# A list scheduler's durations refitted, TensorE's changes of tile shape counted, and strips of two key blocks joined in layers 2 and 3

## The chip, the cores and the metric

The kernel runs on one core of a Trainium2 chip. The metric is the device time of one launch in microseconds, the median of several runs. Everything is computed in float32.

## The reference

A batch of 32 samples x of 512 nodes by 256 features passes through four graph-attention layers. All samples share one 512 x 512 adjacency matrix. Each layer takes h = relu(layernorm(x)) and adds its result to x.

- Layer 0: multi-head attention, 4 heads of 64. Scores q k / 8, masked by the adjacency, softmax, times v, an output projection.
- Layer 1: a linear layer to 512 with relu, a graph attention without mask over 512 features, a linear layer back to 256 with relu, a second graph attention with the mask, elu and relu.
- Layer 2: graph attention with 4 heads of 64. The score of nodes i, j is leaky_relu(s_i + d_j), masked, softmax over j, times the projected features; then elu.
- Layer 3: the same with 8 heads of 32 and a prior beta * log(adj + eps) added to the score, then an output projection.

## The kernel before, in words

**Tiles.** A sample is worked in blocks of 128 partitions x 512 columns of float32. There are 61 such SBUF buffers (`BLOCKS`), 8 PSUM banks, 4 buffers for x, and some small ones. NT = 4 is the number of 128-node blocks, KD = 2 and KH = 4 the numbers of 128-feature blocks of 256 and 512.

**The shapes on TensorE.** Most matmuls use the whole 128 x 128 array, with 512 or 256 to 272 columns streamed. Some use a part of it, several side by side:

- `sc` in layer 0 (scores of two heads): 64 rows each, two side by side, in one unit of two matmuls.
- `av` in layers 0 and 2 (weighted sum of v): 64 output columns each, two side by side.
- `av` in layer 3, `sm` (sums of the softmax's denominators) in layers 0, 2 and 3, and `f1p` in layer 1: 32 output columns each, four side by side.

**Layers 2 and 3** (`separable`): the softmax's numerator of head h, key block j is max(R, e) * mask, one scalar_tensor_tensor on VectorE (512 columns) into a block `p3`; R is the row of the other node's score, broadcast to all partitions by a DMA out of a DRAM tile `rd`, which a DMA before it filled from `rT`. For a group of four heads and one key block j, four such products make a strip. Its four `av` and four `sm` matmuls are one unit.

**The order.** Nothing is issued while the layers are written down. `Plan` records each operation of all 32 samples as a `Step`, with its engine, how long it is taken to keep the engine busy and how long until others can use its result (`cost`), and what must come before it. `with q.unit(busy):` joins several matmuls in one step with a duration of its own. `Plan.order` then lists the steps: again and again it takes, over all five engines, the open step that can start first, ties by `due`, the sample's number times `PERIOD` less the length of what still hangs on the step. A step can start when its engine is free (`at`), its inputs are there (`ready`: the producer's end plus `HOP`) and buffers are free (`slots`). At most 4 samples are in work at once (`AHEAD`). `Plan.issue` issues the steps in this order, each on its engine's queue, so every planned instruction has the line L217 in the profile. At run time each engine goes through its queue in order, with semaphores for what it depends on. The planned durations steer only the order.

**The norm** at the head of each layer (`norm_t`): four bn_stats and bn_aggr on VectorE, a small add, `rs` = (var + eps) ** -0.5 as a pow on POOL, four scalings into `h` on VectorE, eight transposes on TensorE into `pt`, two relu copies on ScalarE into `hT`.

Ahead of the planned part some 100 us go to loading weights, testing bounds and making the masks.

Of the kernel before, what the change touches and what calls it, by code (L numbers as in the profile page):

```python
# [14 lines left out]
ALU = mybir.AluOpType  # L15
# [21 lines left out]
SAFE_PRIOR = 20.0  # L37


PERIOD = 90.0  # L40
BLOCKS, KEEP = 61, 12
KEEP_BANKS = 0

# [1 line left out]
class Step:  # L45


    def __init__(self, engine, busy):
        self.engine, self.busy, self.calls = engine, busy, []
        self.touches, self.before, self.after = [], [], []  # L50


class Plan:
# [6 lines left out]


    ENGINES = dict(tensor="PE", vector="DVE", scalar="ACT", gpsimd="POOL", sync="SP")
    HOP, AHEAD = 0.12, 3

    def __init__(self, nc, period):
        self.nc, self.period = nc, period
# [13 lines left out]
        self.samples.append([])  # L80
        self.history = {}

    def unit(self, busy):

        return _Unit(self, busy)

    def add(self, attribute, engine, op, args, kw):
        steps = self.samples[-1]
# [27 lines left out]
    def order(self):  # L116

        owners, left = {}, {}
        for s, steps in enumerate(self.samples):
            for step in steps:  # L120
                step.sample = s
                step.waits = len(step.before)
                step.ready = 0.0
                for name in step.touches:
                    left[name] = left.get(name, 0) + 1
                    owners[name] = s
            for step in reversed(steps):
                step.tail = step.lasts + max((n.tail + self.HOP for n in step.after), default=0.0)
                step.due = s * self.period - step.tail

                if step.engine != "PE" and any(self.tile_tag[name] == "bank" for name in step.touches):
                    step.due -= 1000.0
        free = {tag: [0.0] * bufs for tag, (bufs, _) in self.tags.items()}
        held = {}
        to_come = [{} for _ in self.samples]
        for name, s in owners.items():
            tag = self.tile_tag[name]
            to_come[s][tag] = to_come[s].get(tag, 0) + 1
        live, at = set(), {e: 0.0 for e in self.ENGINES.values()}
        open_ = {e: [] for e in at}  # L140
        for steps in self.samples:
            for step in steps:
                if not step.waits:
                    open_[step.engine].append(step)
        result, count = [], sum(map(len, self.samples))
        oldest = 0

        def slots(step):

            when, taken = 0.0, {}  # L150
            for name in step.touches:
                if name in live:
                    continue
                tag = self.tile_tag[name]
                keep = self.tags[tag][1]
                reserve = 0
                for s in range(oldest, step.sample):
                    if to_come[s].get(tag, 0):
                        reserve += max(0, min(keep, to_come[s][tag] + held.get((s, tag), 0)) - held.get((s, tag), 0))
                n = taken.get(tag, 0)  # L160
                if len(free[tag]) - n <= reserve:
                    return None
                when = max(when, sorted(free[tag])[n])
                taken[tag] = n + 1
            return when

        while len(result) < count:
            best = None
            for engine, waiting in open_.items():
                for step in waiting:  # L170
                    if step.sample > oldest + self.AHEAD:
                        continue
                    start = max(at[engine], step.ready)
                    if best is not None and self.key(start, step) >= best[0]:
                        continue
                    when = slots(step)
                    if when is None:
                        continue
                    start = max(start, when)
                    if best is None or self.key(start, step) < best[0]:  # L180
                        best = self.key(start, step), start, step
            assert best is not None, "the buffers do not suffice"
            _, start, step = best
            step.start = start
            open_[step.engine].remove(step)
            at[step.engine] = start + step.busy
            end = start + step.lasts
            for name in step.touches:
                tag, s = self.tile_tag[name], step.sample
                if name not in live:  # L190
                    live.add(name)
                    free[tag].remove(min(free[tag]))
                    held[s, tag] = held.get((s, tag), 0) + 1
                    to_come[s][tag] -= 1
                left[name] -= 1
                if not left[name]:
                    live.discard(name)
                    held[s, tag] -= 1
                    free[tag].append(end + self.HOP)
            for n in step.after:  # L200
                n.waits -= 1
                n.ready = max(n.ready, start + step.busy if n.engine == step.engine == "PE" else end + self.HOP)
                if not n.waits:
                    open_[n.engine].append(n)
            result.append(step)
            while oldest < len(self.samples) and not any(to_come[oldest].values()) and not any(
                n for (s, _), n in held.items() if s == oldest
            ):
                oldest += 1
        self.makespan = max(at.values())  # L210
        return result
# [15 lines left out]


class _Unit:
    def __init__(self, plan, busy):  # L230
        self.plan, self.busy = plan, busy

    def __enter__(self):
        self.plan.joined = Step("PE", self.busy)

    def __exit__(self, *_):
        self.plan.joined = None
# [14 lines left out]

def cost(engine, op, args, kw, out):

    n = 1
    for _, k in out.ap[1:]:
        n *= k
    if engine == "PE":
        if op == "transpose":
            return 0.11, 0.2  # L260
        return max(0.22, n * 0.00168), 0.2
    if engine == "ACT":
        return 0.08 + 0.00093 * n, 0.09 + (0.19 if "accum_out" in kw else 0.0)
    if engine == "DVE":
        if op == "reciprocal":
            return 0.07 + 0.00625 * n, 0.09
        return 0.066 + 0.00105 * n + (0.06 if op == "scalar_tensor_tensor" and n == N else 0.0), 0.09
    if engine == "POOL":
        return (1.05 if n < 16 else 0.2 + 0.0015 * n), 0.1
    return 0.1, 3.5  # L270


# [1 line left out]
def gnn_stack_kernel(ctx: ExitStack, tc: tile.TileContext, a: dict, out: bass.AP):  # L274
# [218 lines left out]
    def pipelined(stack):  # L493
# [135 lines left out]
        def layer0(xt):  # L629
# [15 lines left out]
            for m in range(KD):  # L645
                av, sm = bank("av"), bank("sm")
                for jj in range(0, NT, 2):
                    p = {}
                    for j in (jj, jj + 1):
                        sc = [bank("sc"), bank("sc")]  # L650
                        with q.unit(0.96):
                            for s, r in enumerate(rows):
                                q.tensor.matmul(sc[s], kT[m][r, col(j)], qT[m][r, :], start=True, stop=True)
                        for s in range(2):
                            p[j, s] = b = block("p0")
                            q.scalar.activation(b, sc[s], AF.Exp)
                            q.vector.tensor_tensor(b, b, mask0T[:, j, :], op=ALU.mult)
                    with q.unit(2.75):
                        for j in (jj, jj + 1):
                            for s, r in enumerate(rows):  # L660
                                q.tensor.matmul(
# [14 lines left out]
        def first_gat(o1):  # L676
# [3 lines left out]

            part, sd = block("part"), small("sd", NT, 2)
            f1p = bank("f1p")
            with q.unit(1.0):
                for k in range(KH):
                    q.tensor.matmul(f1p[k * 32 : k * 32 + 32, :], fr1a[:, k, :], o1[k], start=True, stop=True)
            q.scalar.copy(part, f1p)
# [116 lines left out]
        def separable(xt, w, nh, mask, bars):  # L803
# [23 lines left out]
            for g in range(nh // 4):  # L827
# [2 lines left out]
                    q.sync.dma_start(R[s], rd[4 * g + s : 4 * g + s + 1, :].to_broadcast([P, N]))  # L830
                avs = [bank("av") for _ in range(4 // per)]
                sm = bank("sm")
                for j in range(NT):
                    p = blocks("p3", 4)
                    for s in range(4):
                        h = 4 * g + s
                        q.vector.scalar_tensor_tensor(
                            p[s], R[s], e[:, j, nh + h : nh + h + 1], mask[:, j, :], op0=ALU.max, op1=ALU.mult
                        )
                    st = dict(start=(j == 0), stop=(j == NT - 1))  # L840
                    with q.unit(1.92 if per == 4 else 2.85):
                        for s in range(4):
                            h, r0 = 4 * g + s, s % per * f
                            q.tensor.matmul(avs[s // per][r0 : r0 + f, :], half(v, j)[:, h * f : (h + 1) * f], p[s], **st)
                        for s in range(4):
                            h = 4 * g + s
                            q.tensor.matmul(
                                sm[s * F3 : (s + 1) * F3, :], wj[:, j, h : h + 1].to_broadcast([P, F3]), p[s], **st
                            )
                bars(g, avs, sm)  # L850

# [457 lines left out]
```

## Time and profile before

| | us |
|---|---|
| median of 3 runs | 4729.1 |
| lowest and highest | 4728.43, 4732.22 |
| the profiled execution's own time | 4727.03 |
| its span, first to last instruction | 4725.2 |
| TensorE busy | 4491.1 |
| VectorE busy | 3061.7 |
| ScalarE busy | 1642.7 |
| POOL busy | 611.8 |

The profile is of one execution. PE is TensorE's matmuls, PEld its weight loads, DVE VectorE, ACT ScalarE, POOL GpSimd and SP the queue that issues the DMAs. A row of the groups names the line, the engine, the operation and its tiles as out<-in with the rows*columns of the array, then the number of instructions; after the bar come the busy time and the mean length of one. A float32 matmul shows as two instructions (two passes), a transpose as one. In the waits, "A <- B" says that A's engine stood idle until B was done.

### The profile page before, as it was taken

How to read it: one execution, taken by the hardware profiler on the slowest of the kernel's cores; microseconds unless marked ns; L12 is line 12 of the kernel's file. 1: busy time of each engine (PE TensorE's matmuls, PEld its weight loads, DVE VectorE, ACT ScalarE, POOL GpSimd, SP SyncE). 2: the span in 40 equal slices, each digit the busy share in tenths (PEclk: the TensorE clock that was granted, in tenths of full speed). 3: DMA queues.
4: the chain of work that ended last, by engine and by line, in shares of the span. 5: the costliest groups of instructions: out<-in, count | busy, mean ns of one | idle time of the engine just before them, and what ended most of it. 6: DMA issues, size and time to landing. Idle time of an engine off the chain costs nothing.

```text
span 4725.2 us, 55985 instructions
## 1 busy us (share of the span) xinstructions
PE 4491.1 (95%) x20146; PEld 2069.3 (44%) x20146; DVE 3061.7 (65%) x6772; ACT 1642.7 (35%) x3508; POOL 611.8 (13%) x648
## 2 busy tenths in 40 slices
PE   2999999999999999999999999999999999999986
PEld 1444444444444444444444444444444444444442
DVE  5357676665667665677657776567666675667664
ACT  1343333333333333333333333333333333333321
POOL 1011111011101111111011110111110111101110
PEclk9999999999999999999999999999999999999997
DMA  2001111101111111111111111111011111111111
GB/s 85 10 18 50 34 46 38 43 30 37 38 40 35 44 39 30 46 44 37 35 36 34 44 46 37 33 38 49 28 44 31 41 42 45 29 39 35 42 36 42
DMA packets 168209, 183.04 MB, mean 39 GB/s; under 512 B 64370, under 2 KB 99956, under 8 KB 167924
## 3 DMA queue, kind: packets, MB, share of 16 engines
q1 hardware_dynamic: 161972, 173.10, 12.1%
q10 hardware_dynamic: 5408, 4.20, 0.3%
q8 instruction: 161, 2.64, 0.2%
q0 software_dynamic: 544, 2.10, 0.1%
q14 instruction: 124, 1.02, 0.1%
HBM read 159.92 MB, written 19.40 MB: 38 GB/s over the span
## 4 chain that ended last, share of the span: by engine, by line
PE 82%; DVE 10%; POOL 2%; ACT 2%; DMA 2%; issue 1%; SPq 0%; POOLq 0%; DVEq 0%; ACTq 0%
PE mm L217 34%; PE av L217 26%; PE sm L217 10%; PE pt L217 6%; PE sc L217 4%; DVE stats L217 2%; DVE x L217 2%; POOL rs L217 1%; DVE p L217 1%; DVE h L217 1%; PE f1p L217 1%; POOL p L217 1%; DVE ue L217 1%; DVE yT L217 1%; ACT e L217 1%
## 5 line engine op out<-in xcount | busy, mean ns | idle before, releaser
L217 PE MATMUL av<-p,v 128*128 128x512 f32 (+1 forms) x2048 | 726.2, 603 | 0.1
L217 DVE SCALAR_TENSOR_TENSOR p<-R,e,mask3T 128x512 f32<-128x512 f32 x1024 | 690.8, 748 | 14.3 <-DMA R<-rd 13.9
L217 PE MATMUL av<-p,vs 128*32 128x512 f32 (+1 forms) x3072 | 555.8, 604 | 14.1 <-DVE p L217 13.4
L217 PE MATMUL mm<-W_fc,o 128*128 128x512 f32 x1024 | 484.7, 602 | 0.0
L217 POOL TENSOR_TENSOR rs<-ve,mhalf 128x4 f32<-128x4 f32 x128 | 172.6, 1351 | 2087.1 <-DVE ve L217 1654.7
L217 PE MATMUL sm<-p,w 128*32 128x512 f32 x3072 | 424.8, 597 | 0.0
L217 DVE TENSOR_TENSOR p<-p,mask0T 128x512 f32<-128x512 f32 x512 | 348.1, 717 | 103.6 <-ACT p L217 102.6
L217 DVE SCALAR_TENSOR_TENSOR p<-R,e,mask1T 128x512 f32<-128x512 f32 x512 | 346.6, 748 | 80.1 <-DMA R<-rd 79.8
L217 ACT ACTIVATE p<-sc 128x512 f32<-128x512 f32 x512 | 274.8, 601 | 349.5 <-PE sc L217 348.0
L217 PEld LDWEIGHTS av<-p,v 128*128 128x128 f32 (+1 forms) x2048 | 243.4, 163 | 319.1 <-issue 274.4
L217 PEld LDWEIGHTS av<-p,vs 128*32 128x32 f32 (+1 forms) x3072 | 125.0, 118 | 369.8 <-issue 207.2
L217 POOL TENSOR_SCALAR p<-p,r 128x512 f32<-128x512 f32 x128 | 140.8, 1110 | 1103.2 <-DVE r L217 736.5
L217 PE MATMUL sc<-qT,kT 64*128 64x512 f32 x1024 | 280.9, 634 | 1.1 <-ACT s L217 0.9
L217 PEld LDWEIGHTS mm<-W_fc,o 128*128 128x128 f32 x1024 | 179.9, 190 | 183.1 <-issue 173.6
L217 PE MATMUL mm<-w,hT 128*128 128x272 f32 (+1 forms) x1024 | 255.8, 396 | 2.2 <-ACT hT L217 1.5
L217 DVE TENSOR_SCALAR h<-x,mv,rs 128x256 f32<-128x256 f32 x512 | 215.8, 475 | 62.0 <-POOL rs L217 61.6
L217 PE MATMUL mm<-o,mlp_w 128*128 128x512 f32 x512 | 235.0, 600 | 8.7 <-DVE o L217 8.7
L217 PE MATMUL pt<-ident,h 128*128 128x128 f32 x1024 | 169.4, 291 | 75.2 <-DVE h L217 73.3
L217 ACT COPY v<-mm 128x512 f32<-128x512 f32 (+1 forms) x256 | 122.7, 479 | 332.9 <-PE mm L217 325.8
L217 PE MATMUL mm<-hT,mlp_w 128*128 128x512 f32 x512 | 237.0, 605 | 0.8 <-ACT hT L217 0.7
L217 PE MATMUL av<-pT,v 128*128 128x512 f32 x512 | 233.3, 594 | 2.1 <-ACT pT L217 2.1
L217 DVE TENSOR_TENSOR vs<-mm,w 128x256 f32<-128x256 f32 x256 | 105.2, 420 | 188.6 <-ACT w L217 185.0
(188 smaller groups left out, 6124.5 us busy)
## 6 DMA issues: line engine op xcount, KB each, us to landing
R<-rd SPq DMA_DIRECT2D x384, 256.0 KB
x<-in_x_dram SPq DMA_DIRECT2D x32, 512.0 KB
rc<-s SPq DMA_DIRECT2D x128, 128.0 KB
rc<-s SPq DMA_DIRECT2D x256, 64.0 KB
out_dram<-x SPq DMA_DIRECT2D x32, 512.0 KB
adj<-in_adj_dram POOLq DMA_DIRECT2D x2, 1024.0 KB, 7.1
s<-sums SPq DMA_DIRECT2D x128, 8.0 KB
few<-s SPq DMA_DIRECT2D x128, 8.0 KB
```

The costliest lines, as they stand in the source:

```text
L217: getattr(getattr(self.nc, attribute), op)(*args, **kw)
```

## The change

It alters five things in the plan and one in the layers. All matmuls, and all operations of the other engines, stay the same in kind and number.

1. A step on TensorE gets a mode: "rows" for the `sc` units, "columns" for the units of `av` and `sm` and of `f1p`, "full" for all else. If a step's mode differs from that of TensorE's step before it, its earliest start is put back by `SWITCH` of the mode that is left. As the earliest start comes first, a step of the present mode is taken ahead of one of another mode that could start as early.
2. `HOP` goes from 0.12 to 0.05, `PERIOD` from 90 to 55.
3. The durations in `cost` are set anew. bn_stats and reduce_max are costed by the length of their input, not of their output; a small POOL operation by 1.3, not 1.05; a PE result can be used 0.165 after its end, not 0.2; others by less.
4. The units' durations are set anew, without what a change of mode costs.
5. In layers 2 and 3 a unit takes two key blocks: eight products, then eight `av` and eight `sm` matmuls in one unit, not four and four.

```diff
-PERIOD = 90.0
+PERIOD = 55.0
...
-    HOP, AHEAD = 0.12, 3
+    HOP, AHEAD = 0.05, 3
+
+    SWITCH = dict(full=0.094, columns=0.12, rows=0.2)
...
                     start = max(at[engine], step.ready)
+                    if engine == "PE" and step.mode != mode:
+                        start = max(start, at[engine] + self.SWITCH[mode])
                     if best is not None and self.key(start, step) >= best[0]:
                         continue
...
             at[step.engine] = start + step.busy
+            if step.engine == "PE":
+                mode = step.mode
...
+    src = args[1] if op in ("bn_stats", "reduce_max") else out
     n = 1
-    for _, k in out.ap[1:]:
+    for _, k in src.ap[1:]:
         n *= k
     if engine == "PE":
         if op == "transpose":
-            return 0.11, 0.2
-        return max(0.22, n * 0.00168), 0.2
+            return 0.109, 0.165
+        return max(0.2, n * 0.001676), 0.165
     if engine == "ACT":
-        return 0.08 + 0.00093 * n, 0.09 + (0.19 if "accum_out" in kw else 0.0)
+        return 0.08 + 0.00095 * n, 0.085 + (0.19 if "accum_out" in kw else 0.0)
     if engine == "DVE":
         if op == "reciprocal":
-            return 0.07 + 0.00625 * n, 0.09
-        return 0.066 + 0.00105 * n + (0.06 if op == "scalar_tensor_tensor" and n == N else 0.0), 0.09
+            return 0.07 + 0.00625 * n, 0.085
+        return 0.066 + 0.00105 * n + (0.06 if op == "scalar_tensor_tensor" and n == N else 0.0), 0.085
     if engine == "POOL":
-        return (1.05 if n < 16 else 0.2 + 0.0015 * n), 0.1
+        return (1.3 if n < 16 else 0.15 + 0.0016 * n), 0.1
     return 0.1, 3.5
...
-                        with q.unit(0.96):
+                        with q.unit("rows", 0.86):
...
-                    with q.unit(2.75):
+                    with q.unit("columns", 2.63):
...
-            with q.unit(1.0):
+            with q.unit("columns", 0.86):
...
-                for j in range(NT):
-                    p = blocks("p3", 4)
-                    for s in range(4):
+                for jj in range(0, NT, 2):
+                    p = {(j, s): block("p3") for j in (jj, jj + 1) for s in range(4)}
+                    for (j, s), b in p.items():
                         h = 4 * g + s
                         q.vector.scalar_tensor_tensor(
-                            p[s], R[s], e[:, j, nh + h : nh + h + 1], mask[:, j, :], op0=ALU.max, op1=ALU.mult
+                            b, R[s], e[:, j, nh + h : nh + h + 1], mask[:, j, :], op0=ALU.max, op1=ALU.mult
                         )
-                    st = dict(start=(j == 0), stop=(j == NT - 1))
-                    with q.unit(1.92 if per == 4 else 2.85):
-                        for s in range(4):
+                    with q.unit("columns", 3.45 if per == 4 else 5.2):
+                        for (j, s), b in p.items():
                             h, r0 = 4 * g + s, s % per * f
-                            q.tensor.matmul(avs[s // per][r0 : r0 + f, :], half(v, j)[:, h * f : (h + 1) * f], p[s], **st)
-                        for s in range(4):
+                            q.tensor.matmul(
+                                avs[s // per][r0 : r0 + f, :], half(v, j)[:, h * f : (h + 1) * f], b,
+                                start=(j == 0), stop=(j == NT - 1),
+                            )
+                        for (j, s), b in p.items():
                             h = 4 * g + s
                             q.tensor.matmul(
-                                sm[s * F3 : (s + 1) * F3, :], wj[:, j, h : h + 1].to_broadcast([P, F3]), p[s], **st
+                                sm[s * F3 : (s + 1) * F3, :], wj[:, j, h : h + 1].to_broadcast([P, F3]), b,
+                                start=(j == 0), stop=(j == NT - 1),
                             )
```

Left out are the class `_Unit` and `Plan.unit`, which pass the mode on, and `Step`, which keeps it.

More of the change, by code (lines that the diff above doesn't have):

```diff
@@ L45, with __init__ @@
 class Step:
-    def __init__(self, engine, busy):
-        self.engine, self.busy, self.calls = engine, busy, []
+    def __init__(self, engine, busy, mode="full"):
+        self.engine, self.busy, self.mode, self.calls = engine, busy, mode, []
         self.touches, self.before, self.after = [], [], []
@@ L81, in begin, with unit @@
         self.history = {}
-    def unit(self, busy):
-        return _Unit(self, busy)
+    def unit(self, mode, busy):
+        return _Unit(self, mode, busy)
     def add(self, attribute, engine, op, args, kw):
@@ L144, in order @@
                     open_[step.engine].append(step)
-        result, count = [], sum(map(len, self.samples))
+        result, count, mode = [], sum(map(len, self.samples)), "full"
         oldest = 0
@@ L229, with __init__ @@
 class _Unit:
-    def __init__(self, plan, busy):
-        self.plan, self.busy = plan, busy
+    def __init__(self, plan, mode, busy):
+        self.plan, self.step = plan, Step("PE", busy, mode)
     def __enter__(self):
-        self.plan.joined = Step("PE", self.busy)
+        self.plan.joined = self.step
     def __exit__(self, *_):
```

## The prediction, made before the changed kernel was run

> **What bounds the kernel now.** I read the page first, then TensorE's timeline in one stretch of the steady part, then its waits, then the chain of waits. The page:
>
> ```profile
> span 4725.2 us, 55985 instructions
> PE 4491.1 (95%) x20146; PEld 2069.3 (44%) x20146; DVE 3061.7 (65%) x6772; ACT 1642.7 (35%) x3508; POOL 611.8 (13%) x648
> PE   2999999999999999999999999999999999999986
> PE 82%; DVE 10%; POOL 2%; ACT 2%; DMA 2%; issue 1%; SPq 0%; POOLq 0%; DVEq 0%; ACTq 0%
> ```
>
> TensorE is busy in 95% of the span, from the third slice to the last but one, and holds 82% of the chain. No other engine passes 65%. So the time is what TensorE must do, plus the holes in it. Busy does not say whether it runs at its rate: a 512-wide pass shows 602 ns, yet passes start every 430 ns. The timeline of TensorE tells (first number: start; second: length; a float32 matmul shows as two passes):
>
> ```profile
> 2056.80 1.02 PE L217 MATMUL mm<-hT,wqT 128*128 128x512 f32 x2
> 2057.66 1.02 PE L217 MATMUL mm<-hT,wkT 128*128 128x512 f32 x2
> ...
> 2347.47 1.94 PE L217 MATMUL av<-p,v 128*64 128x512 f32 x8
> 2349.34 1.06 PE L217 MATMUL sm<-p,ones 128*32 128x512 f32 x8
> 2350.34 3.32 PE L217 MATMUL mm<-W_hand,o 128*128 128x258 f32 x14
> ...
> 2356.53 0.59 PE L217 MATMUL mm<-wvT,hT 128*128 128x256 f32 x2
> 2357.06 1.13 PE L217 MATMUL sc<-qT,kT 64*128 64x512 f32 x4
> 2358.11 2.00 PE L217 MATMUL mm<-wvT,hT 128*128 128x256 f32 x8
> ...
> 2362.16 1.99 PE L217 MATMUL sc<-qT,kT 64*128 64x512 f32 x8
> 2364.08 0.70 PE L217 MATMUL mm<-L_WoT,oT 128*128 128x256 f32 x2
> ```
>
> Subtract starts. Two full-array passes: 0.86, so 0.43 each. The sc passes run two side by side: x4 should take 0.86 and takes 1.05, x8 should take 1.72 and takes 1.92: **0.20 per visit, however long**. The 64-column av passes: 1.87 for 4 x 0.43 = 1.72, so 0.15. The 32-column sm passes, four side by side: 1.00 for 0.86, so 0.14. Full-array work before a change of shape: 0.53 for 2 x 0.215, so 0.10. Medians over the whole trace, per run of one shape: full 0.094, 32 columns 0.139, 64 columns 0.155, 64 rows 0.202, the one-row matmul 0.043 us. Transposes with 4 or 8 output rows show no such cost (187 of them go on to full-array work after 109 ns), so I count them as full.
>
> The waits of TensorE (total us, times, longest):
>
> ```profile
> PE pt L217 <- DVE h L217: 73.3, 44, 24.3
> PE mm L217 <- ACT hT L217: 18.0, 11, 2.6
> PE pt L217 <- POOL p L217: 16.7, 14, 6.9
> PE mm L217 <- DVE oT L217: 16.4, 2, 9.9
> PE av L217 <- DVE p L217: 13.4, 2, 6.8
> PE mm L217 <- DVE o L217: 8.7, 6, 1.4
> ```
>
> 24.3 us of the first row is the start. Asked for 110 to 4400 us alone, the waits sum to 76 us, 35.1 of them pt for h; after 4400 us they sum to 59 us.
>
> **What the Trainium skill says.** "TensorEngine Tiling (Array Packing)", section Tiling Modes: changing the tiling mode, not just the tile, drains TensorE. It gives no price; this trace agrees and prices it, as above. "Perfetto Trace Analysis", Identifying the Most-Contended Engine: matmul occupancy is no good measure, since matmuls are pipelined; it agrees (602 ns shown, 430 ns apart), so I count starts. "TensorE: Matmul & The Clock Gate", Part 1: idle gaps of some microseconds lower TensorE's clock; the granted clock is 0.99 to 1.00 up to 4410 us and 0.79 in the last 66 us, where gaps reach 9.9 us. So a gap closed at the end is worth a little more than its length.
>
> **The sum of before.** One sample holds 64 full-array 512-wide matmuls x 0.858 = 54.9, 48 of 256 to 272 columns x 0.44 = 21, 16 sc x 0.429 = 6.9, 32 of 64 columns x 0.429 = 13.7, 100 of 32 columns x 0.2145 = 21.4, 89 transposes x 0.109 = 9.7 and 1.3 of tiny ones: 128.9 us, 4,130 for 32 samples. I counted runs of one shape in the order that the program was built to issue: 425 full, 424 of 32 columns, 256 of 64, 218 of 64 rows, 32 of one row: 40.0 + 58.9 + 39.7 + 44.0 + 1.4 = 184 us. Ahead of the first planned matmul lie 108 us, after the last 5. That leaves 4725 - 108 - 5 - 4130 - 184 = about 298 us in holes: some 16 in the first 300 us, 96 after 4400, the rest even. The chain shows the same piece (mm, x26) at 2053.51 and 2620.72, four samples apart: 141.8 us a sample, against 128.9 + 184/32 = 134.7; so 7 us of holes a sample. Only a third shows as idle: a hole shorter than a matmul's tail (about 170 ns) is covered by it.
>
> **The change part by part.** The matmuls are the same; their order isn't.
>
> 1. Shape changes. In the built order of after I count 182 full runs, 251 of 32 columns, 192 of 64, 78 of 64 rows, 32 of one row: 17.1 + 34.9 + 29.8 + 15.8 + 1.4 = 99 us. **-85 us**, on TensorE and so on the path. Joining explains part: layer 2 has 64 fewer visits to 64 columns (64 x 0.155 = 10 us); the rest is the list that now picks work of the present shape. Bounds: prices hold within 10%, -77 to -93.
>
> 2. Durations. The old costs took the length of bn_stats from its 6 outputs (0.07 us); the trace has 182.0/512 = 0.36. The pow on POOL was planned at 1.05, the trace has 1.35. So each norm was planned over a microsecond short, four times a sample, and pt for h leads the waits. The new costs say 0.33 and 1.3. The built order shows the effect: TensorE work placed between a sample's last instruction before a norm and its first transpose of h (samples 6 to 26, least/middle): layer 1 6.2/10.0, now 6.6/20.2; layer 2 5.1/5.9, now 6.0/7.5; layer 3 7.8/9.5, now 10.3/20.8. Between the last transpose of e and layer 3's first strip: 12.2/12.7, now 19.5/22.9. In the steady part, intervals into pt of h, mm of hT, mlp2's mm and pt of p exceed their price by 85 us in 20 samples, so about 119 in 28. I let two fifths go: **-50**. Bounds: -119 if all goes, and +45, for the hand-over was also cut, HOP from 0.12 to 0.05 and the tail of TensorE from 0.2 to 0.165. In the trace a strip's product ends and its weight load starts 0.09 us later, the matmul about 0.15; the plan now gives 0.135. If a third of some 60 hand-overs a sample is late by 0.07, that is 45 us. Still too short are the layer-0 mask product (0.604 planned, 348.1/512 = 0.68) and the POOL product (0.97 planned, 1.11).
>
> 3. Joined strips. A unit now waits for eight products of VectorE, not four: 4 x 0.675 = 2.7 us later. Behind it in TensorE's queue stands everything placed after it. In the steady part 20 us of other work lie ahead of it, so nothing; with that cover gone it costs 2.7 a group, 3 groups a sample. At the end the last sample has no cover: 3 to 8 us there, with the last unit running 1.7 us longer after its last product.
>
> 4. The end. In the old order the last sample has the final 48 us of TensorE work alone, in the new one 35 (sample 30 keeps 11 us to put into its gaps). **-10** net of step 3; bounds -25 and +15. The start: sample 0 takes turns with 1 to 3, where before it led; TensorE was 100% busy there anyway: 0, within 10 either way.
>
> DMAs are the same in number; SP's list order moves with the plan, R's loads included, and the longer distance above covers them. VectorE, ScalarE and POOL have room (65, 35, 13%).
>
> Sum against the profiled execution (4727.0 us, span 4725.2): 4727 - 85 - 50 - 10 = 4582. The median of the runs, 4729.1, is 2 higher: **4584 us**.
>
> **The rivals.** (a) The changes of shape go but the holes stay, or new short ones take their place: for it speaks that the hand-over was cut; against, the longer distances. 4729 - 85 = 4644; 20%. (b) Nearly all the waits of step 2 go and the end gains 25: 4729 - 85 - 119 - 25 = 4500; 15%. (c) Slower: four joined strips of layer 3 now stand in a row (runs of 64 column matmuls, 64 x 0.2145 = 13.7 us), and VectorE needs 32 x 0.675 = 21.6 us for their products, beside other samples' work. If R lands late, or VectorE is taken, TensorE stands in that run and all behind it. It decides from 85/32 = 2.7 us a sample; at 5 us it gives 4729 - 85 + 160 = 4804. For it: nothing lies between the strips any more. Against: 19.5 us or more ahead of the run, VectorE at 65%. 5%. That the change doesn't do what it says is excluded for the shapes by the built order; for the durations it is (a).
>
> **How the numbers follow.** The main case has 60%, by itself 4540 to 4625. With (b) and most of (a) the range is 4515 to 4650. A measurement of this kernel tells about 0.2%, 9 us, from no change (its runs lie within 0.08%). Faster by more: 0.94 (main, b, nearly all of a). Within: 0.02. Slower: 0.04 (c).
>
> **What would show it.** Right: sc, av and sm in longer pieces in TensorE's timeline, with the same 0.14 to 0.20 per run; a period of 135 to 138 us a sample; pt for h well under 35 us between 110 and 4400 us. Step 2 is wrong if the period stays over 139; step 4 if the holes after the last 330 us stay near 96. The prediction fails if av for p (DVE) appears among the steady waits with more than 2.7 us a sample, or if a run of one shape costs another price in the new order.

## The result and the profile after

The changed kernel takes **4552.2 us** (median of 4 runs, 4551.29 to 4553.7) against 4729.1: ratio 0.9625, 95% interval 0.9608 to 0.9642. That is 177 us off, where 145 were forecast; it lies inside the stated range.

The page of the changed kernel (planned instructions now have the line L223):

```profile
span 4550.1 us, 55600 instructions
PE 4372.6 (96%) x20146; PEld 2143.5 (47%) x20146; DVE 3042.0 (67%) x6772; ACT 1622.5 (36%) x3508; POOL 571.0 (13%) x648
PE   2999999999999999999999999999999999999996
PE 90%; DVE 5%; DMA 2%; ACT 1%; issue 1%; POOL 0%; SPq 0%; ACTq 0%; POOLq 0%; DVEq 0%
```

PE, PEld, DVE, ACT and POOL have as many instructions as before. TensorE's share of the chain rose from 82% to 90%: what went out of the chain is mostly other engines' work that TensorE had stood waiting for. Its timeline in the steady part:

```profile
2299.14 1.90 PE L223 MATMUL av<-p,vs 128*32 128x512 f32 x16
2300.85 1.90 PE L223 MATMUL sm<-p,w 128*32 128x512 f32 x16
2302.68 2.85 PE L223 MATMUL sc<-qT,kT 64*128 64x512 f32 x12
2305.46 1.92 PE L223 MATMUL av<-p,vs 128*32 128x512 f32 x16
...
2309.03 1.94 PE L223 MATMUL av<-p,v 128*64 128x512 f32 x8
2310.90 1.06 PE L223 MATMUL sm<-p,ones 128*32 128x512 f32 x8
2311.89 1.94 PE L223 MATMUL av<-p,v 128*64 128x512 f32 x8
```

Subtract starts again. An av of 32 columns with an sm of 32 columns behind it, so without a change, takes 1.71 for 16 passes, four side by side: 4 x 0.43, nothing more. The sc visit takes 2.78 for 12 passes, 6 x 0.43 and the same 0.20 as the visits of 4 and 8 did before. The 64-column av takes 1.87 and the sm 0.99, as before. So the price of a run is what it was, and there are fewer runs: 735 instead of 1355.

The waits of TensorE between 110 and 4230 us (total us, times, longest):

```profile
PE pt L223 <- DVE h L223: 5.1, 5, 3.4
PE av L223 <- DVE p L223: 4.0, 13, 0.6
PE mm L223 <- ACT hT L223: 3.9, 10, 0.7
PE sc L223 <- ACT p L223: 3.8, 5, 0.8
```

Before, pt for h alone had 35.1 us between 110 and 4400 us. In the chain the same piece returns after five samples:

```profile
1512.22 23.20 PE mm L223 x62
2184.81 23.20 PE mm L223 x62
```

672.6 / 5 = 134.5 us a sample, against 141.8.

To compare many kernels I take the trace apart in one way. Each start-to-start interval on TensorE has a price (0.43 for a 512-wide pass, and so on, with the change of shape); what it takes beyond that is a **hole**. Holes are summed over the start (the first 590 us from the first planned matmul), the end (the last 340) and the middle. "Shapes" is the number of runs of each shape times its price.

A hole so counted is not all waiting. After some waits the granted clock falls to 0.5 for 3.4 us or a small multiple of it (up to 17.1), and 512-wide passes then start 0.85 us apart, not 0.43. From the granted clock in the two traces I estimate that this makes 14 of the 179 us in the middle before and 2 of the 68 after, none of the 29 at the start before and 7 of the 52 after, and 13 and 20 of the 97 at the end.

| kernel | median us | shapes | holes: start | middle | end |
|---|---|---|---|---|---|
| before | 4729.1 | 184 | 29 | 179 | 97 |
| after | 4552.2 | 99 | 52 | 68 | 97 |
| before + SWITCH alone | 4662.5 | 108 | 26 | 178 | 112 |
| before + durations alone | 4653.2 | 187 | 32 | 96 | 102 |
| after, SWITCH 0 | 4618.0 | 151 | 22 | 113 | 97 |
| after, durations as before | 4603.7 | 101 | 38 | 124 | 98 |
| after, single strips | 4506.8 | 105 | 40 | 46 | 82 |
| after, HOP 0.12 | 4544.3 | 111 | 19 | 83 | 94 |
| single strips, HOP 0.12 | 4505.2 | 114 | 24 | 51 | 79 |
| after, PERIOD 90 | 4554.0 | 94 | 44 | 99 | 70 |
| single strips, PERIOD 90 | 4651.5 | 119 | 45 | 138 | 113 |
| after, two durations corrected | 4503.9 | 90 | 29 | 55 | 94 |
| single strips, corrected | 4492.3 | 105 | 22 | 45 | 82 |
| single strips, corrected, PERIOD 60 | 4627.5 | 105 | 34 | 157 | 96 |

The columns of shapes and holes are of the profiled execution; for "after, PERIOD 90" that one took 4543.4 us, 11 under the median.

From before to after: shapes -85, middle -111, start +23, end 0, together -173 of the 177.

### The profile page after: what moved, and what is told of

It reads as the page before. It is cut to its first block, busy times and chain, and to the rows that moved or that the text cites. A ratio compares the mean times of both kernels' runs of the same rounds, so it can differ in the third digit from the quotient of the medians.

```text
span 4550.1 us, 55600 instructions
## 1 busy us (share of the span) xinstructions
PE 4372.6 (96%) x20146; PEld 2143.5 (47%) x20146; DVE 3042.0 (67%) x6772; ACT 1622.5 (36%) x3508; POOL 571.0 (13%) x648
## 4 chain that ended last, share of the span: by engine, by line
PE 90%; DVE 5%; DMA 2%; ACT 1%; issue 1%; POOL 0%; SPq 0%; ACTq 0%; POOLq 0%; DVEq 0%
PE mm L223 39%; PE av L223 29%; PE sm L223 10%; PE pt L223 7%; PE sc L223 4%; DVE p L223 3%; PE f1p L223 1%; DVE s L223 0%; PE fb L223 0%; POOL p L223 0%; DMA R<-rd 0%; DVE ue L223 0%; ACT hT L223 0%; DVE stats L223 0%; DMA beta<-in_beta_dram 0%
## 5 line engine op out<-in xcount | busy, mean ns | idle before, releaser
L223 PE MATMUL av<-p,v 128*64 128x512 f32 (+1 forms) x2048 | 718.9, 603 | 3.0 <-DVE p L223 3.0
L223 DVE SCALAR_TENSOR_TENSOR p<-R,e,mask3T 128x512 f32<-128x512 f32 x1024 | 710.3, 761 | 5.3 <-DMA R<-rd 5.3
L223 PE MATMUL av<-p,vs 128*32 128x512 f32 (+1 forms) x3072 | 510.3, 597 | 16.1 <-DVE p L223 16.0
L223 POOL TENSOR_TENSOR rs<-ve,mhalf 128x4 f32<-128x4 f32 x128 | 156.9, 1226 | 2725.9 <-DVE ve L223 2297.1
L223 PE MATMUL mm<-W_fc,o 128*128 128x512 f32 x1024 | 457.3, 592 | 0.0
L223 PEld LDWEIGHTS av<-p,v 128*64 128x64 f32 (+1 forms) x2048 | 249.1, 164 | 375.1 <-issue 323.4
L223 DVE SCALAR_TENSOR_TENSOR p<-R,e,mask1T 128x512 f32<-128x512 f32 x512 | 345.7, 744 | 59.4 <-DMA R<-rd 59.2
L223 DVE TENSOR_TENSOR p<-p,mask0T 128x512 f32<-128x512 f32 x512 | 327.5, 689 | 83.3 <-ACT p L223 83.3
L223 PE MATMUL sm<-p,w 128*32 128x512 f32 x3072 | 377.7, 594 | 0.0
L223 ACT COPY sums<-sm 128x512 f32<-128x512 f32 x128 | 75.0, 586 | 699.0 <-PE sm L223 650.3
L223 ACT ACTIVATE p<-sc 128x512 f32<-128x512 f32 x512 | 262.7, 633 | 101.2 <-PE sc L223 100.6
L223 PEld LDWEIGHTS av<-p,vs 128*32 128x32 f32 (+1 forms) x3072 | 137.3, 119 | 341.4 <-issue 258.0
L223 DVE TENSOR_TENSOR vs<-mm,w 128x256 f32<-128x256 f32 x256 | 103.9, 420 | 286.1 <-ACT w L223 276.2
L223 PEld LDWEIGHTS mm<-W_fc,o 128*128 128x128 f32 x1024 | 191.2, 190 | 206.0 <-issue 195.3
L223 PE MATMUL mm<-w,hT 128*128 128x272 f32 (+1 forms) x1024 | 280.8, 403 | 5.6 <-ACT hT L223 3.2
L223 ACT COPY v<-mm 128x512 f32<-128x512 f32 (+1 forms) x256 | 123.1, 481 | 428.5 <-PE mm L223 417.1
L223 DVE TENSOR_SCALAR h<-x,mv,rs 128x256 f32<-128x256 f32 x512 | 213.6, 474 | 87.6 <-POOL rs L223 87.2
L223 PE MATMUL sc<-qT,kT 64*128 64x512 f32 x1024 | 252.2, 607 | 4.2 <-ACT p L223 3.8
L223 PE MATMUL mm<-hT,mlp_w 128*128 128x512 f32 x512 | 233.9, 593 | 0.4 <-ACT hT L223 0.3
L223 PE MATMUL mm<-o,mlp_w 128*128 128x512 f32 x512 | 231.2, 594 | 0.6 <-DVE o L223 0.6
L223 PE MATMUL av<-pT,v 128*128 128x512 f32 x512 | 229.0, 600 | 0.1
L223 PEld LDWEIGHTS mm<-w,hT 128*128 128x128 f32 x1024 | 193.1, 197 | 74.8 <-issue 23.1
```

The costliest lines, as they stand in the source:

```text
L223: getattr(getattr(self.nc, attribute), op)(*args, **kw)
```

## The experiments

**1. SWITCH alone.** Modes and SWITCH put into the kernel before; all durations, HOP, PERIOD and strips as they were.

```diff
+    SWITCH = dict(full=0.094, columns=0.12, rows=0.2)
...
+                    if engine == "PE" and step.mode != mode:
+                        start = max(start, at[engine] + self.SWITCH[mode])
```

> The kernel before with the mode of a step and SWITCH alone; durations, HOP 0.12, PERIOD 90 and single strips as before. Its built order has 801 runs of one shape (162 full, 308 of 32 columns, 256 of 64, 43 of 64 rows, 32 of one row), 108 us at the prices of the trace, against 184 before and 99 after. Theory (shapes and waits are two separate gains; the waits follow the planned durations): 76 us off, the steady holes stay at 6 to 8 us a sample, 4653 us. Rival (the waits fell because work of one shape now stands together and gives each chain more room): the steady holes fall here too, to 3 us a sample, and the time is 4540 to 4580.

Measured 4662.5 us, ratio 0.9857 (0.9841 to 0.9874). The shapes fall by 76 us, the middle's holes stay at 178, the end's grow by 15. The waits between 700 and 4320 us still begin with the norm:

```profile
PE pt L223 <- DVE h L223: 24.9, 30, 2.2
PE pt L223 <- POOL p L223: 17.8, 11, 3.4
```

The theory is within 10 us. The rival falls: the middle's holes stayed, so longer runs of one shape did not close the waits.

**2. The new durations alone.** Only the function `cost` is exchanged in the kernel before.

```diff
+    src = args[1] if op in ("bn_stats", "reduce_max") else out
...
-        return (1.05 if n < 16 else 0.2 + 0.0015 * n), 0.1
+        return (1.3 if n < 16 else 0.15 + 0.0016 * n), 0.1
```

> The kernel before with the new durations in cost alone (bn_stats by its input, POOL's pow 1.3, TensorE's tail 0.165); no modes, HOP 0.12, PERIOD 90, single strips. Its built order has 1419 runs, 187 us at the trace's prices, 3 more than before. Theory (the waits follow the planned durations): steady holes fall from 7 to about 3 us a sample, 30 samples, so 4729 - 115 + 3 = 4617 us, and pt for h leaves the head of the steady waits. Rival (room from runs of one shape, or HOP and PERIOD): holes stay, 4725 to 4735.

Measured 4653.2 us, ratio 0.9837 (0.982 to 0.9853). The middle's holes fall from 179 to 96, those before pt of h from 60 to 10. Between 700 and 4300 us the longest waits are now:

```profile
PE mm L217 <- ACT hT L217: 5.1, 10, 1.8
PE av L217 <- ACT s L217: 5.0, 7, 0.7
```

The mechanism is the forecast one; the size is 83 us, not 115. Some 11 us of new holes at layer 2's and 3's av are part of the shortfall; the rest was not traced. Steps 1 and 2 alone give 67 and 76 us; they add up to 143 of the 177.

**3. SWITCH taken out of the changed kernel.**

```diff
-    SWITCH = dict(full=0.094, columns=0.12, rows=0.2)
+    SWITCH = dict(full=0.0, columns=0.0, rows=0.0)
```

> The changed kernel with SWITCH all zero: durations, HOP, PERIOD, joined strips kept. Its built order has 1175 runs, 151 us at the trace's prices, 52 more than the changed kernel. Theory: 4552 + 52 = 4604 us with holes of 2 to 3 us a sample as in the changed kernel; as the plan no longer knows the changes of shape, it runs ahead of TensorE, which leaves more room, so not more holes. Rival (room comes from runs of one shape): holes go back to 6 to 7 us a sample, some 4700 us.

Measured 4618.0 us, ratio 0.9761 (0.9745 to 0.9777). Shapes +52 as counted, but the middle's holes grow by 45 (before mm of hT alone from 5 to 50) while the start's fall by 30. So "not more holes" was wrong, and the full rival, 4700, as well.

**4. The old durations in the changed kernel.**

```diff
-    src = args[1] if op in ("bn_stats", "reduce_max") else out
...
-        return (1.3 if n < 16 else 0.15 + 0.0016 * n), 0.1
+        return (1.05 if n < 16 else 0.2 + 0.0015 * n), 0.1
```

> The changed kernel with the durations in cost as before (bn_stats by its output, pow 1.05, TensorE's tail 0.2); modes, SWITCH, HOP 0.05, PERIOD 55, joined strips and the units' new durations kept. 754 runs of one shape, 101 us at the trace's prices, 2 more than the changed kernel. Theory (the durations of the other engines' steps close the steady holes): steady holes back at 5 to 7 us a sample with pt for h at their head, 4552 + 2 + 60 to 120 = 4615 to 4675 us. Rival (units and modes do it, the durations are by the way): 4545 to 4560.

Measured 4603.7 us, ratio 0.9735 (0.9719 to 0.9752), 51 us over the changed kernel. The middle's holes go from 68 to 124, and the norm is back at the head of the waits (700 to 4250 us):

```profile
PE pt L223 <- DVE h L223: 21.6, 40, 1.5
PE pt L223 <- POOL p L223: 12.3, 8, 1.6
```

The rival falls. The time is 11 us under the expected 4615 to 4675: the middle has 56 us more holes, but the start has 14 fewer. With experiment 2 this shows from both sides that the new `cost` closed the norm's wait, and the other kernels agree: in the middle, pt of h has 60, 50 and 40 us of holes in the three kernels with the old durations (before, experiments 1 and 4) and 12 or less in all eleven with the new ones. `cost` was only exchanged as a whole, so which of its entries did it is argued, not shown. bn_stats, planned at 0.07 us and taking 0.36, is the likeliest.

**5. Single strips.** The changed kernel with four products and eight matmuls to a unit.

```diff
-                for jj in range(0, NT, 2):
-                    p = {(j, s): block("p3") for j in (jj, jj + 1) for s in range(4)}
+                for jj in range(NT):
+                    p = {(jj, s): block("p3") for s in range(4)}
...
-                    with q.unit("columns", 3.45 if per == 4 else 5.2):
+                    with q.unit("columns", 1.73 if per == 4 else 2.6):
```

> The changed kernel with strips of one key block (units of 1.73 and 2.6). Its built order has 774 runs, 104.7 us at the trace's prices, 5.8 more than the changed kernel. Theory: joining is worth these 6 us in the steady part, and costs some at start and end, where TensorE stands in a unit and follows VectorE's products one by one: 4552 + 6 - 0 to 20, so 4540 to 4558 us. Rival (joining carries much of the gain): 4580 us or more.

Measured 4506.8 us, ratio 0.9524 (0.9508 to 0.954): **45 us faster** than the changed kernel. Shapes +6 as counted, but the holes are 49 us fewer, in all three parts. Neither expectation held. Two readings were left: joining makes holes by what it is, or its order is unlucky. The start of the changed kernel speaks for the first, with VectorE's products coming one by one:

```profile
478.82 1.04 PE L223 MATMUL av<-p,vs 128*32 128x512 f32 x2 [0.60 <-DVE p L223]
480.14 1.04 PE L223 MATMUL av<-p,vs 128*32 128x512 f32 x2 [0.28 <-DVE p L223]
481.47 1.47 PE L223 MATMUL av<-p,vs 128*32 128x512 f32 x9 [0.28 <-DVE p L223]
```

Two products come every 1.33 us, 0.665 each, and TensorE stands inside its unit between them.

**6. and 7. HOP 0.12, joined and single.**

```diff
-    HOP, AHEAD = 0.05, 3
+    HOP, AHEAD = 0.12, 3
```

> The changed kernel (joined strips) with HOP back at 0.12. Its built order has 830 runs of one shape, 111 us at the trace's prices, 12 more than the changed kernel. If the cut of HOP bought nothing in waits, 4552 + 12 = 4564 us; if the cut made new short waits (my bound of 45 us for late hand-overs), 4520 to 4555; if the shorter HOP is itself what closed the steady holes, 4600 or more.

> Single strips (as in the run without joining, 4507 us) with HOP 0.12. 854 runs, 114 us, 9 more than single strips with 0.05. Theory A (joining makes holes by what it is: TensorE bound to a unit that needs eight products): single strips stay 30 to 60 us under the joined kernel at this HOP too. Theory B (the list falls into one of many orders, and joining was unlucky once): the difference between joined and single changes its size or sign. By shapes alone 4516 us.

Measured 4544.3 us, ratio 0.9606 (0.959 to 0.9622), and 4505.2 us, ratio 0.9524 (0.9508 to 0.954). Joined: shapes +12, start -33, middle +15. The total fell where late hand-overs would have put it, but not for that reason: in both pairs the middle has more holes with the long hand-over, not fewer (83 against 68, 51 against 46). Of the 45 us that I had allowed for late hand-overs nothing is seen. Single strips are 39 us under joined, so theory A still stood.

**8. and 9. PERIOD 90, joined and single.**

```diff
-PERIOD = 55.0
+PERIOD = 90.0
```

> The changed kernel (joined) with PERIOD back at 90. 708 runs, 94 us, 5 fewer than the changed kernel. If PERIOD 55 only made the start worse (52 us of holes in the first 590 us, against 29 before), the start falls to about 30 and the time is 4552 - 5 - 22 = 4525; if 55 is what lets steady holes close, 4570 or more.

> Single strips with PERIOD 90. 872 runs, 119 us, 14 more than single strips with 55: 4507 + 14 = 4521 us by shapes alone. Theory A: 30 to 60 us under the joined kernel with PERIOD 90. Theory B: no fixed sign; by the start alone (40 us of holes with 55) up to 10 us less.

Measured 4554.0 us, ratio 0.9629 (0.9613 to 0.9645), and 4651.5 us, ratio 0.9836 (0.9819 to 0.9852). Now **joined is 97 us under single**. Theory A falls. Neither expectation for the joined kernel held: the start shrank to 44, not 30, so PERIOD 55 alone did not lengthen it, and the middle's holes grew by 31. The single one shows that the new durations do not by themselves make a good order: its middle has 138 us of holes, more than with the old durations in experiment 4, though pt of h waits only 3.6 us there (700 to 4310 us). The waits that the trace names there sum to 33 us, 7.8 for the longest entry; where the rest lies was not traced.

**10. and 11. Two more durations corrected, joined and single.** The trace of before has 348.1/512 = 0.68 us for layer 0's mask product and 1.11 for POOL's product, planned at 0.60 and 0.97. The edit reaches further than these two: it sets every 512-wide tensor_tensor of VectorE and every longer operation of POOL, among them POOL's 512-wide step on e, which takes 0.72 us and is now planned at 1.12.

```diff
-... (0.06 if op == "scalar_tensor_tensor" and n == N else 0.0), 0.085
+... (0.06 if op == "scalar_tensor_tensor" and n == N else 0.07 if op == "tensor_tensor" and n == N else 0.0), 0.085
...
-        return (1.3 if n < 16 else 0.15 + 0.0016 * n), 0.1
+        return (1.3 if n < 16 else 0.3 + 0.0016 * n), 0.1
```

> The changed kernel, joined, with the same two durations set right. 681 runs, 90 us, 9 fewer than the changed kernel. By shapes 4543; with the start's 52 us of holes back at 25 to 30, 4515 to 4525. If joining by itself held TensorE up, it stays at 4540 or over.

> Single strips, HOP 0.05, PERIOD 55, and two durations that the trace of before shows too short set right: 512-wide tensor_tensor on VectorE 0.67, not 0.60, and POOL's 512-wide products 1.12, not 0.97. 774 runs, 104.5 us, as in the single-strip run (4507 us). If what is left of steady holes (46 us) comes of durations still too short, 4475 to 4500; if they are at their floor, 4500 to 4512; if the new list falls otherwise, any sign up to 40.

Measured 4503.9 us joined, ratio 0.9522 (0.9506 to 0.9538), and **4492.3 us** single, ratio 0.9499 (0.9484 to 0.9515), the best of all. Joined gains 48 us (start -23, middle -13, shapes -9), single 14 (start -18, the middle 46 and 45). So the single one landed in the range for steady holes that close, but these did not close; the gain lies at the start, and the hit is luck. Joining is now 12 us behind. In the best kernel TensorE has 97% of the span and 94% of the chain:

```profile
PE 4334.5 (97%) x20146; PEld 2121.5 (47%) x20146; DVE 3028.5 (67%) x6772; ACT 1609.1 (36%) x3508; POOL 526.1 (12%) x648
PE 94%; DVE 2%; DMA 1%; issue 1%; ACT 1%; POOL 0%; SPq 0%; ACTq 0%; POOLq 0%; DVEq 0%
```

**12. PERIOD 60 instead of 55** in that kernel, and nothing else.

```diff
-PERIOD = 55.0
+PERIOD = 60.0
```

> The single-strip kernel with the two durations set right and PERIOD 60, not 55: nothing else. 775 runs, 104.7 us, the same as with 55 within 0.2 us. If PERIOD acts smoothly, the time is within 10 us of the run with 55; if the list falls into one of many orders whose holes differ by chance, it may differ by 30 to 100 us with no change in shapes.

Measured 4627.5 us, ratio 0.9779 (0.9762 to 0.9795): **135 us slower** with the same shapes to 0.2 us. The chain of waits with PERIOD 55, and then with PERIOD 60:

```profile
1456.85 8.58 PE mm L223 x20
1590.37 8.58 PE mm L223 x20
```

```profile
2067.57 19.76 PE mm L223 x52
2164.34 12.06 DVE p L223 x17
2344.02 19.76 PE mm L223 x52
2440.80 12.06 DVE p L223 x17
```

With 55 the order repeats every sample, 133.5 us; with 60 every two samples, 276.5, 138.2 each, with VectorE's p on the chain in each turn. TensorE's timeline shows where it is lost:

```profile
2248.27 0.38 PE L223 MATMUL pt<-mx,ones 1*128 1x1 f32 x2
2250.50 0.65 PE L223 MATMUL pt<-ident,ew 128*128 128x128 f32 x4 [1.86 <-ACT ew L223]
2252.77 7.44 PE L223 MATMUL av<-p,v 128*128 128x512 f32 x10 [1.61 <-DVE p L223]
```

ScalarE at the same time:

```profile
2248.79 1.56 ACT L223 ACTIVATE ue<-ue 128x256 f32<-128x256 f32 x4 [4.82 <-DVE ue L223]
2250.26 0.19 ACT L223 ACTIVATE ew<-ew 128x4 f32<-128x4 f32 x1
```

VectorE:

```profile
2248.68 0.16 DVE L223 COPY nd<-pt 128x1 f32<-128x1 f32 x1
...
2248.85 1.06 DVE L223 TENSOR_TENSOR ue<-pt,r 128x256 f32<-128x256 f32 x3
2249.82 0.22 DVE L223 TENSOR_SCALAR ew<-sd,nd 128x4 f32<-128x4 f32 x1
```

Layer 1's first attention has a chain of small steps (mx, nd, ew, r, p). In this order the tiny ew stands behind layer 2's steps on ue, about 1 us on VectorE and 0.2 us behind their exponentials on ScalarE, so pt of ew starts 2.1 us after the last pt of mx, where it is 1.1 us in the kernel with 55. And TensorE has nothing placed between pt of mx, pt of ew and av, where with 55 it has 12 passes of other work. After this wait the granted clock is halved:

```profile
2248.00:2252.00 4.00, 1.30 (x10) 0.80 (x7) 3.95 (x18) 2.55 (x8) 0.00 (x0) 0.98 0.40 137
2252.00:2258.00 6.00, 5.23 (x6) 2.18 (x7) 5.46 (x13) 0.00 (x0) 0.00 (x0) 0.50 0.25 84
```

(From and to, then the busy time of PE, PEld, DVE, ACT and POOL, then the clock: 0.98 and 0.50.) The ten passes of av take 7.27 us to the next start, where 10 x 0.43 are due. Of some 6.5 us lost here every second sample about half is the wait and about half the slow clock; together that is more than 3 of the 4.7 us a sample between the two orders. A small step of PERIOD put this in, and it comes back 12 times because the order settles into a cycle.

So theory B holds: HOP, PERIOD, joining and small durations each send the greedy list into another order, and which one decides over as much as 135 us with the same shapes. No single run tells the worth of such a setting.

## Why the prediction was right or wrong

**Step 1, shapes, -85: right.** 735 runs in the trace, the prices unchanged. SWITCH by itself gave 76 us of shapes and 67 of time.

**Step 2, durations, -50: the mechanism right, the term too small.** The middle's holes fell by 111. I let two fifths of the intervals before pt of h, mm of hT, mlp2's mm and pt of p go. In the middle they went from 60, 20, 13 and 13 us to 7, 5, under 1 and 6: over four fifths. The bound I held against it, 45 us for late hand-overs, did not show: with HOP back at 0.12 the middle had 83 us of holes, with 0.05 it had 68. Two fifths was a guess without a working, so that the sum came near is in part luck. Two readings behind the step were off. The 1.35 us of the pow is a mean: its median is 1.04, as the old plan had it, so in more than half of the norms bn_stats was the whole shortfall. And the clock of 0.99 to 1.00 up to 4410 us, read over 300 to 1000 us at a time, hid nine falls to 0.5 of 3.4 us each, which went with the waits; after, there is one.

**Step 3, joining, nothing in the steady part: not wrong as a count, but the wrong question.** The 2.7 us for eight products were covered in the steady part, and at the start TensorE did stand in the unit. What joining does depends on which order the list falls into: joined less single is +45, +39, -97 and +12 us in four pairs.

**Step 4, the end, -10: wrong; the start, 0 within 10: wrong.** The end's holes stayed at 97 with the last sample alone for 35 instead of 48 us of work. The waits changed place; the last sample's layer 3 still has them (the longest single ones, in the last 320 us):

```profile
PE pt L223 <- DVE h L223: 12.4, 2, 7.7
PE mm L223 <- DVE oT L223: 9.0, 2, 7.4
```

From the first transpose of its layer 3 to the end it takes 59.7 us before and 60.1 after, and 58.5 to 60.6 in all fourteen kernels: the order did not shorten that chain, joined or not. The step had put the end's price on how much work the last sample has alone.

The start's holes grew from 29 to 52 us. They come after the first 300 us, which the prediction read, when the four first samples, started together, reach layers 2 and 3, where VectorE binds. In the slice from 410 to 510 us VectorE is busy for 81 us of 100, TensorE for 93, and the chain runs over VectorE:

```profile
477.44 16.66 DVE p L223 x26
```

It is this order's doing: the same work has 19 to 29 us of holes there with SWITCH 0, with HOP 0.12 and with the two durations corrected.

The errors: 61 us too little in step 2, against 10 and 23 us at the ends; together 28 of the 32 us between forecast and result. Errors of both signs met in that sum, and the forecast is nearer than its terms. (A slip in the sum of before: 128.9 x 32 is 4,125, not 4,130, which leaves 303 us of holes; the table has 305.)

**The rivals.** (a), holes stay, fell: they went from 305 to 217. (b), nearly all waits of step 2 go, was right for the middle and wrong for the end, and its 4500 us lie 52 under the result. (c), joined runs late for want of products, did not decide: av for p shows 4.0 us in all between 110 and 4230 us, where 2.7 a sample were needed. Of the signs named, the pieces, the prices and pt for h came as stated, and 97 us of holes at the end said that step 4 was wrong; the 134.5 us a sample are just under the 135 to 138 given.

**What stays open.** Why a given setting falls into a good cycle was seen in one place (experiment 12) and not followed in the others. Experiment 3's new wait before mm of hT, the holes of single strips at PERIOD 90, and the cost of joining at PERIOD 55 may be of the same kind; that is not shown. As a setting moves the time by up to 135 us through the order alone, the times of experiments 1 to 4 are draws too; what carries them is where the holes went, not the totals. The last 34 of the 177 us, beyond what steps 1 and 2 give alone, belong to HOP, PERIOD, joining, the units' durations and their interplay, and were not taken apart.

## What to carry to other kernels

Price a change of TensorE's tile shape from start-to-start distances, count the runs in the built order, and that part of the gain can be told in advance (with SWITCH alone 76 us counted, 67 measured). Check a planner's durations against the trace row by row, above all operations whose output is much smaller than their input, and small operations in a chain, by the median and not the mean alone: here the new durations closed nearly half of the steady holes by themselves (179 to 96 us). A greedy list is jumpy: judge a setting by several neighbours and by where the holes lie, and look for a tiny step queued behind bulk work of another sample, and for the clock after it.

## What the runs showed of the hardware that had not been expected

A visit to the 64-row shape has a price that does not depend on its length: 0.20 us with 4, 8 or 12 passes (1.05, 1.92, 2.78 us), and half of it lies inside, between the first pair and the second (0.53 us from start to start, not 0.43). Transposes with 1, 4 or 8 output rows cost no change at all: full-array work follows 109 ns later in the 187 cases of the trace before.

A wait in the middle of the run can cost twice. In experiment 12 TensorE had two waits of 1.86 and 1.61 us with four transposes between them; from the second on the granted clock stood at 0.5 for 6.8 us, and the passes of av started 0.85 us apart, not 0.43.
